# Reordering a planned kernel: layer 2 of the first pair ahead of layer 0's last pass, priorities in time, and quarter sums made by transfers

## The chip, the cores and the metric

The kernel runs on one core of a Trainium2 chip. The metric is device time in microseconds (us) of one execution, as a median of several. A core has a matrix engine (TensorE, PE in the profile; its weight loads are PEld), three engines for element-wise work (VectorE = DVE, ScalarE = ACT, GpSimd = POOL) and SyncE (SP), which in this kernel issues transfers. Each engine works off its own list of instructions in order and waits for others by semaphores. Transfers that SP issues and transfers that POOL issues stand in two separate queues and share 16 DMA engines.

## The reference

Four graph layers over x (8 batches x 2048 nodes x 64 channels) and one row-normalised adjacency matrix A (2048 x 2048, f32); each layer's output is added to its input and normalised over the channels. Cut to what matters:

```python
# layer 0: Chebyshev products, weights by node
y1 = A @ x;  y2 = 2 * (A @ y1) - x
out = sum over k in 0..2, d in 0..15 of emb[n, d] * ([x, y1, y2][k] @ w[d, k]) + bias
# layer 1: graph attention
e = leaky_relu(s1[:, None] + s2[None, :]);  e = where(A > 0.5, e, -9e15)
out = elu(softmax(e) @ x)
# layer 2
out = ((A + I) @ (x @ W.T + b)) / rowsum(A + I)
# layer 3: v = x with node 0 set to a constant, then three times
v = relu([v, A @ v] @ W1.T + b1) @ W2.T + b2
```

Attention is a dense 2048 x 2048 softmax for each batch, so its element-wise work is large; the products with A are 2048 x 2048 by 512 columns each.

## The kernel before, in words

**Tiling.** The 8 batches make 4 *pairs* p = 0..3 of two batches, 128 columns of x each. A pair's x lies in SBUF as `SX[p]`, 16 node tiles of 128 x 128. Three more slots of that size, `SA`, `SB` and `SH`, hold y1, then u, h and results; `SH` holds layer 0's weights first. A product with A is a *sweep*: for each of 4 column chunks `c` (512 nodes) and 8 steps `q`, a tile `a` (128 x 2 x 512, 512 KB) of the transposed A is loaded, and two matmuls of 512 columns are accumulated on a PSUM bank `acc` (L1093). So a sweep is 32 tiles and 64 matmuls of a pair. SP issues the tile loads in the fixed order of the list `order_of_a` through a ring of six buffers (`fetch`, L234 to L245); `plus` takes tiles with the identity added, for layer 2.

**Stages.** Layer 0: `first_product` gives y1, `second_product` gives y2 (evicted by `y2_evict`), and `second_pass` (L576) does the matmuls with all 16 weight blocks (yp, L601), which `add_terms` (L613) weighs and sums on ACT and DVE; `first_norm` ends it. The sweep of pair 0's and 1's first products also makes the 0/-9e15 masks of A, which are stored (`by_col`, `by_row`). Layer 1: `layer1` and `scores` (L700) find the largest score of each row, `weights` (L798) makes the exponentials for one node tile: an add on DVE (L809), leaky ReLU on ACT (L817), an add on DVE (L822), an exp on ACT (L825), and then the matmul with x on PE (po, L836). POOL loads the masks for it (`mk`, `mr`). `finish` (L853, matmul pf L870) divides, applies elu and normalises; half 0 is staged and copied to `SX` by a POOL transfer. Layer 2: a sweep `layer2_product`, evicted to z by `z_evict` (L942, L945), then for each chunk `layer2_tail` (ps_emb L981 on PE, adds L990 and L994 on DVE), `start_chunk` (norm, transpose ps_vT L1015 into `SH`) and `u_chunk` (ps_u L1028, into `u_of(p, s)`). These tails wait in a queue, `queue2`, which `tails` works off in order. Layer 3: three sweeps over u, each with one seed matmul a chunk (L1082) and a relu eviction (`h_evict`, L951), then `u_chunk` or, in the end, `last_chunk` (ps_v L1048) and `store` (L1064).

**Joint layers.** Pairs 2 and 3 go together. `joint_layer2` (L1188) uses each `a` tile for both pairs; `sums` (L1159) meanwhile adds quarters of A on DVE (L1172: four sums s1..s4 of 8 tiles each, 32 adds), stored by POOL (L1174, `s<-s`), with some plain tiles loaded again (`pure`). `joint_layer3` (L1247) multiplies the 2x2 blocks of A by the two pairs' u with seven block products in place of eight: `sums_of_u` makes sums of u, `combine` sums of the results, the matmuls are L1299.

**What sets the order.** No loop nest does: the class `Plan` (L38) interleaves generators ("threads"). A thread yields an engine and what it waits for; `go` picks the thread that could begin first by the plan's own estimates of time, ties by rank, and lets it emit its next instructions. For PE a thread is taken to begin `SLACK` = 1.0 us later than its inputs are there. The order so found is fixed in each engine's list when the program is built. `sweeps` (L1404) is the thread of the products: first products of pairs 0 and 1; then for each pair its second product (with the next pair's first product beside it); then for pairs 0 and 1 layer 2 and three steps of layer 3; then the joint layers. `tails` starts once pair 3 has left layer 0:

```python
def tails():
    yield "PE", [("x1", NPAIR - 1)]
    for n in range(NPAIR * 4 * NCH):
        yield "PE", [("q2", n + 1)]
        yield from queue2[n]()
```

Attention of pairs 0, 1, 2, 3 runs beside all this from about 400 us on: the masks' first load is issued at 396.7 us, the last at 1603.1.

Of the kernel before, what the change touches and what calls it, by code (L numbers as in the profile page):

```python
# [12 lines left out]
ALU = mybir.AluOpType  # L13
# [24 lines left out]
class Plan:  # L38
# [7 lines left out]
    SLACK = 1.0  # L46
# [27 lines left out]
    def start(self, rank, gen):  # L74
        try:
            self.threads.append([rank, next(self.count), gen, next(gen)])
        except StopIteration:
            pass
# [11 lines left out]
    def go(self):  # L90
        while self.threads:
            best = min(
                self.threads,
                key=lambda th: (self.begins(th)[0], (*th[3][2:], th[0])[0], th[1]),
            )
            t, _, eng = self.begins(best)
            assert t < NEVER, [th[3] for th in self.threads]
            try:
                best[3] = best[2].send(eng)
            except StopIteration:  # L100
                self.threads.remove(best)
# [42 lines left out]
def resnorm_d4_kernel(  # L144
# [60 lines left out]
    def batches(v):  # L205

        if len(v.shape) == 3:
            v = v.rearrange("p t n -> p (t n)")
        return v.rearrange("p (b c) -> p b c", c=C)

# [116 lines left out]
    for e in range(2):  # L327
# [20 lines left out]
        for m in ("s1", "s2", "s3", "s4")  # L348
# [73 lines left out]
    def rows_of_adj():  # L422


        for t in range(NT):
            yield "SP", [115.0 + 9.0 * t, bc_ring]
# [3 lines left out]
            done = plan.dma("SP", 1024, bc_ring.t, 115.0 + 9.0 * t)  # L430
            plan.start(1, row_tile(t, an, k, done))

    def row_tile(t, an, k, done):
# [15 lines left out]
        if all(("by_row", i) in at for i in range(NT)):  # L449
            at["rows"] = done  # L450
# [125 lines left out]
    def second_pass():  # L576

        for n in range(NPAIR * NCH):
# [32 lines left out]
            xg_ring.give(kx, t_pe)  # L611

# [46 lines left out]
    def layer1(p):  # L659
# [38 lines left out]
        plan.start(10 + p, scores(p, sv, xc, s_rows, done))  # L698

    def scores(p, sv, xc, s_rows, done):  # L700
        s2b = []
        for e in range(2):
            yield "DMA", [bc_ring, done, "rows"]
# [228 lines left out]
    JOINT = (NPAIR - 2, NPAIR - 1)  # L932
    SH_of = {p: SH for p in range(NPAIR)}

    def after_l2(p):
        return SB if p == 0 else SX[p - 1] if p < NPAIR - 1 else SX[0]

    def u_of(p, s):

        return SX[p] if s == 1 else SB if p == NPAIR - 1 else SA  # L940

    def z_evict(p, c, pa, give, done):  # L942
# [4 lines left out]
        give(done)  # L947
# [23 lines left out]
    def tails():  # L971
        yield "PE", [("x1", NPAIR - 1)]
# [28 lines left out]
    def start_chunk(p, c, v, done):  # L1001
# [10 lines left out]
        yield "PE", [done, pp_ring]  # L1012
# [11 lines left out]
    def u_chunk(p, c, w, dst, bias, s, done):  # L1024
        yield "PE", [done, pp_ring]
# [48 lines left out]
    def sweep(*products, masks=False):  # L1074

        for c in range(NCH):
            pas = []
            for source, evict, need, before, seed in products:
                yield "PE", [acc_ring, *before(c)]
                pas.append(acc_ring.take([P, CW], "acc"))  # L1080
                if seed:
                    nc.tensor.matmul(  # L1082
                        pas[-1][0], lhsT=seed, rhs=SH[:, tiles(c), :], start=True, stop=False
# [44 lines left out]

    RQ = AQ // 2

    def quarters(k, r):

        return [(k, r), (k, r + RQ), (k + 2, r), (k + 2, r + RQ)]

    def order_of_joint():
        for k in range(2):
            for r in range(RQ):
                order_of_a.extend((c, q, True) for c, q in quarters(k, r))
        for s in range(3):
            for m in ("a11", "a12", "s2", "s3", "a22", "s1", "s4"):  # L1140
                i, j = {"a11": (0, 0), "a12": (0, 1), "a22": (1, 1)}.get(m, (0, 0))
                for k in range(2):
                    for r in range(RQ):
                        if m[0] == "a":
                            order_of_a.append((k + 2 * i, r + RQ * j, False))
                        else:
                            order_of_a.append((m, (k, r), False))

    def pure(k, r):

        yield "SP", [("group", k, r), *([xg_ring] if len(xg_ring.freed) > 1 else [NEVER])]
        got = []
        for c, q in (quarters(k, r)[i] for i in (0, 3)):
            t, kt = xg_ring.take([P, 2, CW], "pure")
            nc.sync.dma_start(t, tile_of_adj(c, q))
            got.append((t, kt, plan.dma("SP", 512, xg_ring.t)))
        return got

    def sums(k, r, taken):  # L1159

        tiles4 = [(t, kt, got) for t, kt, got, _ in taken]
        own = {}
        if r // 2 == k:
            own = dict(zip((0, 3), (yield from pure(k, r))))
        a11, a12, a21, a22 = ((own.get(i) or tiles4[i])[0] for i in range(4))
        ready = [(own.get(i) or tiles4[i])[2] for i in range(4)]

        def out_of(m, a, b, op, *after):
            yield "DVE", [bc_ring, *after]
            t, kt = bc_ring.take([P, 2, HALF], m)  # L1170
            t = t.rearrange("p a b -> p (a b)")[:, 0 : 2 * CW].rearrange("p (t n) -> p t n", n=CW)
            nc.vector.tensor_tensor(t, a, b, op)  # L1172
            done = plan.run("DVE", dve(2 * CW), *after)
            nc.gpsimd.dma_start(sum_tiles[m][k, r], t)  # L1174
            bc_ring.give(kt, plan.dma("DMA", 512, done))
            return t, done

        s3, d3 = yield from out_of("s3", a11, a21, ALU.subtract, ready[0], ready[2])
        s1, d1 = yield from out_of("s1", a21, a22, ALU.add, ready[2], ready[3])
        s2, d2 = yield from out_of("s2", s1, a11, ALU.subtract, d1)  # L1180
        s4, d4 = yield from out_of("s4", a12, s2, ALU.subtract, d2)
        for (_, kt, _, free), d in zip(taken, (d2, d4, d1, d1)):
            a_ring.give(kt, max(free, d))
        for _, kt, _ in own.values():
            xg_ring.give(kt, d2)
        refill()

    def joint_layer2():  # L1188
        p, o = JOINT
        at["group", 0, 0] = 0.0  # L1190
        for k in range(2):
            pas = {}
            for r in range(RQ):
                taken = []
                for i, (c, q) in enumerate(quarters(k, r)):
                    n = next(used)
                    if r == 0 and i in (0, 2):
                        if i == 0:
                            yield "PE", [po_ring, ("x2", p), ("x2", o)]
                            t2, kp = po_ring.take([P, 2, CW], "po")  # L1200
                            pas[c] = [(t2[:, e, :], kp) for e in range(2)]
                        else:
                            pas[c] = []
                            for e in range(2):
                                yield "PE", [acc_ring]
                                pas[c].append(acc_ring.take([P, CW], "acc"))
                    for e, pair in enumerate(JOINT):
                        yield "PE", [("a", n)]
                        t, kt = a_tiles[n]
                        for b in range(2):  # L1210
                            m = 2 * q + b
                            nc.tensor.matmul(
                                pas[c][e][0],
                                lhsT=SX[pair][:, m, :],
                                rhs=t[:, b, :],
                                start=(r == 0 and i in (0, 2) and b == 0),
                                stop=(r == RQ - 1 and i in (1, 3) and b == 1),
                            )
                        done = plan.run("PE", mm(CW, 2), ("a", n))
                        if r == RQ - 1 and i in (1, 3):  # L1220
                            if i == 3:
                                give = lambda t, kk=pas[c][e][1]: acc_ring.give(kk, t)
                            else:
                                give = give_half(pas[c][e][1])
                            plan.start(1, z_evict(pair, c, pas[c][e][0], give, done))
                    del a_tiles[n]
                    taken.append((t, kt, at["a", n], done))
                    if i == 0:
                        nxt = (k, r + 1) if r + 1 < RQ else (k + 1, 0)
                        at[("group", *nxt)] = plan.free["PE"]  # L1230
                    spent[0] += 1
                plan.start(5, sums(k, r, taken))
                refill()

    halves_left = {}

    def give_half(kp):
        def give(t):
            left, last = halves_left.pop(kp, (2, 0.0))
            if left == 1:  # L1240
                po_ring.give(kp, max(t, last))
            else:
                halves_left[kp] = (1, max(t, last))

        return give

    def joint_layer3():  # L1247
        p, o = JOINT
        U, _ = e_ring.take([P, 2, HALF], "u23")
        T12, _ = e_ring.take([P, 2, HALF], "t12")  # L1250
        T34, _ = e_ring.take([P, 2, HALF], "t34")
        T = [
            t[:, i, :].rearrange("p (t n) -> p t n", n=P) for t in (T12, T34) for i in range(2)
        ]
        for s in range(3):
            up, uo = u_of(p, s), u_of(o, s)
            B11, B21, B12, B22 = up[:, 0:8], up[:, 8:16], uo[:, 0:8], uo[:, 8:16]
            plan.start(0, sums_of_u(s, T, B11, B21, B12, B22))
            u = lambda pair, half: lambda k: ("u", pair, s, 2 * half + k)
            t = lambda i: lambda k: ("t", s, i, k)  # L1260
            seed = gv if s else w31v
            held = {}
# [215 lines left out]
```

## Time and profile before

The times are 2131.99, 2132.62 and 2137.06 us. The page is of one execution of its own:

| | |
|---|---|
| median of 3 runs | 2132.62 us |
| the profiled execution, its time | 2133.99 us |
| its span (first to last instruction) | 2132.2 us |
| mean granted TensorE clock in it | 0.994 |
| PE busy | 97% of the span |
| DVE, ACT, POOL busy | 70%, 46%, 10% |
| moved by transfers | 495.85 MB, mean 233 GB/s |

How to read it: the page's first part gives each engine's busy time, share and number of instructions; its second cuts the span in 40 slices of 53.3 us with one digit each (tenths busy; for PEclk tenths of the full clock). A window line gives, for a stretch of the span, the busy us of each engine in it, the granted clock, the share of the DMA engines' time and GB/s. A wait line names the waiting engine and its line, the engine and line that released it, and the total, number and longest of these waits. A transfer's line ends with the median time from issue to landing. A busy PE is not PE at its peak, and the engines' names of tiles are the program's.

### The profile page before, as it was taken

The page shows a single profiled execution, that of the slowest core. Times are in us where ns is not written, and L with a number is a line of the kernel's source. Part 1 is how long each engine was busy: PE and PEld are TensorE (multiplying, and loading weights), DVE is VectorE, ACT ScalarE, POOL GpSimd, SP SyncE. Part 2 cuts the span into 40 slices and gives each one's busy share as a digit, 9 for nine tenths or more (in the row PEclk, how much of TensorE's full clock was granted, in tenths as well). Part 3 has the DMA queues.
Part 4 walks back from the last instruction along what each step waited for, and adds up shares of the span by engine and source line. Part 5 has one row for each costly group of instructions (what it writes and reads, how often), then busy time and mean ns, then how long its engine had stood idle before and what let it go on. Part 6 is the DMA issues. An engine that isn't in the chain of part 4 may idle for free. (4 is left out here: it accounts for less than half of the span.)

```text
span 2132.2 us, 19037 instructions
## 1 busy us (share of the span) xinstructions
PE 2067.3 (97%) x6325; PEld 914.9 (43%) x6325; DVE 1496.4 (70%) x1908; ACT 974.9 (46%) x1794; POOL 213.0 (10%) x374
## 2 busy tenths in 40 slices
PE   8999999999999999999798999989999999999998
PEld 3444444433433443433343453443444444444444
DVE  2226647998799999789998979999796455120214
ACT  0025424567776566777624857336575012000002
POOL 2310000100110100000010101011010110000000
PEclk9999999999999999999899999999999999999999
DMA  9799835634443465554388778897776777878785
GB/s 303 267 333 345 306 105 209 218 122 136 138 137 131 159 238 169 170 178 150 124 309 299 254 267 285 279 339 239 264 236 234 290 255 273 280 254 281 251 288 188
DMA packets 208740, 495.85 MB, mean 233 GB/s; under 512 B 20274, under 2 KB 28594, under 8 KB 204530
## 3 DMA queue, kind: packets, MB, share of 16 engines
q1 hardware_dynamic: 165058, 347.62, 48.0%
q0 software_dynamic: 39360, 144.92, 19.7%
q10 hardware_dynamic: 4224, 2.10, 0.4%
q8 instruction: 50, 0.82, 0.2%
q14 instruction: 48, 0.39, 0.1%
HBM read 446.14 MB, written 46.33 MB: 231 GB/s over the span
## 5 line engine op out<-in xcount | busy, mean ns | idle before, releaser
L1093 PE MATMUL acc<-a,SX 128*128 128x512 f32 x1024 | 465.8, 598 | 9.6 <-DMA SX<-in_x 6.6
L1093 PE MATMUL acc<-a,SA 128*128 128x512 f32 x768 | 348.6, 596 | 13.1 <-DMA a<-in_adj_t 12.4
L817 ACT ACTIVATE e<-e,sv 128x1024 f32<-128x1024 f32 x256 | 280.1, 1154 | 114.4 <-DVE e L809 110.6
L731 DVE CUSTOM_DVE_ANT_0 junk<-s2b,mr 128x2048 bf16<-128x2048 f32 x128 | 292.7, 2287 | 5.2 <-DMA mr<-by_row 3.9
L624 ACT ACTIVATE terms<-yp,emb_sb 128x128 f32<-128x128 f32 x896 | 243.5, 400 | 113.6 <-PE yp L601 113.3
L1093 PEld LDWEIGHTS acc<-a,SX 128*128 128x128 f32 x1024 | 190.3, 191 | 242.2 <-issue 229.6
L822 DVE TENSOR_TENSOR e<-e,mb 128x2048 f32<-128x2048 f32 x128 | 290.0, 2286 | 6.0 <-ACT e L817 5.4
L809 DVE TENSOR_TENSOR e<-s1b,mk 128x2048 f32<-128x2048 f32 x128 | 289.1, 2286 | 6.5 <-PE po L836 4.0
L825 ACT ACTIVATE e<-e 128x2048 f32<-128x2048 f32 x128 | 245.0, 1928 | 67.5 <-DVE e L822 67.2
L601 PE MATMUL yp<-SH,xgT 128*128 128x512 f32 x512 | 246.9, 607 | 3.3 <-ACT sv L358 3.3
L836 PE MATMUL po<-e,SX 128*64 128x512 f32 x1024 | 235.4, 602 | 3.1 <-ACT e L825 3.1
L1093 PEld LDWEIGHTS acc<-a,SA 128*128 128x128 f32 x768 | 140.9, 190 | 186.0 <-issue 166.0
L1299 PE MATMUL acc<-a,t 128*128 128x512 f32 x384 | 168.7, 592 | 0.0
L636 DVE TENSOR_TENSOR terms<-terms 128x512 f32<-128x512 f32 (+1 forms) x176 | 130.0, 738 | 42.2 <-ACT terms L624 38.2
L601 PEld LDWEIGHTS yp<-SH,xgT 128*128 128x128 f32 x512 | 90.9, 189 | 145.7 <-issue 137.6
L836 PEld LDWEIGHTS po<-e,SX 128*64 128x64 f32 x1024 | 68.1, 137 | 155.8 <-issue 133.7
L601 PE MATMUL yp<-SH,y2T 64*128 64x512 f32 x512 | 128.3, 617 | 0.0
L804 POOL DMA_DIRECT2D mk<-by_col x128 | 69.0, 540 | 546.7 <-DVE e L809 452.1
L1093 PE MATMUL acc<-a,SB 128*128 128x512 f32 x256 | 118.3, 595 | 0.0
L1299 PEld LDWEIGHTS acc<-a,t 128*128 128x128 f32 x384 | 72.0, 190 | 86.1 <-issue 86.1
L601 PEld LDWEIGHTS yp<-SH,y2T 64*128 64x128 f32 x512 | 43.6, 186 | 79.9 <-issue 76.4
L1093 PEld LDWEIGHTS acc<-a,SB 128*128 128x128 f32 x256 | 47.2, 190 | 57.3 <-issue 57.3
(225 smaller groups left out, 1677.7 us busy)
## 6 DMA issues: line engine op xcount, KB each, us to landing
a<-in_adj_t SPq DMA_DIRECT2D x496, 512.0 KB, 5.5
a<-s SPq DMA_DIRECT2D x96, 512.0 KB, 4.5
mr<-by_row POOLq DMA_DIRECT2D x64, 512.0 KB, 5.9
mk<-by_col POOLq DMA_DIRECT2D x128, 256.0 KB, 5.0
an<-in_adj SPq DMA_DIRECT2D x16, 1024.0 KB, 10.7
s<-s POOLq DMA_DIRECT2D x32, 512.0 KB, 5.0
a<-a_plus_i SPq DMA_DIRECT2D x24, 512.0 KB, 5.0
by_col<-mk POOLq DMA_DIRECT2D x32, 256.0 KB, 5.8
```

What stands on the lines that cost most here:

```text
L601: nc.tensor.matmul(yp[:, e, :], lhsT=y2T[rows, cs] if k2 else xg[:, e, cs], rhs=(wk2 if k2 else w01)[rows, hs], start=(k2 == h), stop=(k2 ...
L624: nc.scalar.activation(batches(terms[0][:, dd, :]), term, AF.Copy, scale=weight)
L636: nc.vector.tensor_tensor(a, a, b, ALU.add)
L731: nc.vector.tensor_tensor_reduce(out=junk, in0=s2b[e][0], in1=masks[t][0], scale=1.0, scalar=LOWEST, op0=ALU.add, op1=ALU.max, accum_out=m ...
L804: nc.gpsimd.dma_start(mk, by_col[jt // 2][:, jt % 2, h * HALF : (h + 1) * HALF])
L809: nc.vector.tensor_tensor(e, s1b[0], mk.unsqueeze(1).to_broadcast([P, 2, HALF]), ALU.add)
L817: nc.scalar.activation(e[:, i, :], e[:, i, :], AF.Prelu, bias=sv[:, 2 + i, jt : jt + 1], alpha=ALPHA)
L822: nc.vector.tensor_tensor(e, e, mb[0], ALU.add)
L825: nc.scalar.activation(e, e, AF.Exp)
L836: nc.tensor.matmul(po[i * C : (i + 1) * C, f, :], lhsT=SX[p][:, t, i * C : (i + 1) * C], rhs=e[:, i, f * CW : (f + 1) * CW], start=(t == 0 ...
L1093: nc.tensor.matmul(pa, lhsT=source[:, m, :], rhs=t[:, i, :], start=(m == 0 and not seed), stop=(m == NT - 1),)
L1299: nc.tensor.matmul(pa, lhsT=B[:, 2 * r + b, :], rhs=at_[:, b, :], start=(r == 0 and b == 0 and not go_on), stop=(r == RQ - 1 and b == 1), ...
```

## The change

- **Planner.** `SLACK` is 0.0. A table `BACK` adds a time to a thread's beginning when the next one is chosen (below zero: it goes ahead): `add_terms` of pair 0 by -3.02, `finish` by -0.48, `scores` of pair 2 by -0.01. `scores` gets rank 1.2 for pair 0 and 9.5 + p else, and no longer waits for all rows' masks. The loads of A's rows begin at 120 in place of 115 on the plan's clock.
- **Layer 2 of pair 0** goes ahead of the second product of pair 3. `tails` waits for nothing at its start. Pair 0 gets other slots: its `SH_of` is `SX[0]`, its u goes to `SB`, `SH` and `SB` for the three steps, its layer 2 result to `SA`, with waits until these are free (`x1 used`, `y1 used`, `w0 used`).
- **Joint layer 2** is gone: pairs 2 and 3 have plain sweeps, each loading its own tiles.
- **Quarter sums** (sa = a12 + a22, sb = a11 + a12, sc = sa + a11, sd = sc + a21) are made from DRAM to DRAM by transfers of POOL, planned from 320 us on with 14 us between them: for each of 8 tiles a copy, then a transfer that adds to what is there.
- **Joint layer 3** uses another scheme of seven products on these sums; two products go on in a bank that already holds another, one seed is added to a bank after DVE has read it, and some sums of u are made in place. The matmuls are now at L1219, the seeds at L1203.

```diff
-    SLACK = 1.0
+    SLACK = 0.0
+    BACK = {
+        ("add_terms", 0): -3.02,
+        ("finish", None): -0.48,
+        ("scores", 2): -0.01,
+    }
...
-                key=lambda th: (self.begins(th)[0], (*th[3][2:], th[0])[0], th[1]),
+                key=lambda th: (self.begins(th)[0] + th[4], (*th[3][2:], th[0])[0], th[1]),
...
-            yield "SP", [115.0 + 9.0 * t, bc_ring]
+            yield "SP", [120.0 + 9.0 * t, bc_ring]
...
-        plan.start(10 + p, scores(p, sv, xc, s_rows, done))
+        plan.start(1.2 if p == 0 else 9.5 + p, scores(p, sv, xc, s_rows, done))
...
-            yield "DMA", [bc_ring, done, "rows"]
+            yield "DMA", [bc_ring, done]
...
-    JOINT = (NPAIR - 2, NPAIR - 1)
-    SH_of = {p: SH for p in range(NPAIR)}
+    JOINT = (NPAIR - 1, NPAIR - 2)
+    SH_of = {p: SH if p else SX[0] for p in range(NPAIR)}
     def after_l2(p):
-        return SB if p == 0 else SX[p - 1] if p < NPAIR - 1 else SX[0]
+        return SA if p == 0 else SX[p - 1] if p < NPAIR - 1 else SX[0]
     def u_of(p, s):
-        return SX[p] if s == 1 else SB if p == NPAIR - 1 else SA
+        if s == 1:
+            return SX[p] if p else SH
+        return SB if p in (0, 1, NPAIR - 1) else SA
...
     def tails():
-        yield "PE", [("x1", NPAIR - 1)]
...
     def u_chunk(p, c, w, dst, bias, s, done):
-        yield "PE", [done, pp_ring]
+        room = {0: ["y1 used"], 1: ["w0 used"]}.get(s, []) if p == 0 else []
+        yield "PE", [done, pp_ring, *room]
...
+    QUARTER = {"a11": (0, 0), "a12": (0, RQ), "a21": (2, 0), "a22": (2, RQ)}
+    def sums_of_a():
+        n = itertools.count()
+        for m, a, b in (
+            ("sa", "a12", "a22"),
+            ("sb", "a11", "a12"),
+            ("sc", "sa", "a11"),
+            ("sd", "sc", "a21"),
+        ):
+            for x in (a, b):
+                for k, r in sum_tiles[m]:
+                    if x in QUARTER:
+                        part = tile_of_adj(k + QUARTER[x][0], r + QUARTER[x][1])
+                    else:
+                        part = sum_tiles[x][k, r]
+                    before = [("sum", m, k, r)] if x == b else []
+                    if x not in QUARTER:
+                        before.append(("sum", x, k, r, True))
+                    yield "DMA", [320.0 + 14.0 * next(n), *before]
+                    nc.gpsimd.dma_start(
+                        sum_tiles[m][k, r], part, **({"accum_op": ALU.add} if x == b else {})
+                    )
...
-    def sums(k, r, taken):
...
-            nc.vector.tensor_tensor(t, a, b, op)
-            nc.gpsimd.dma_start(sum_tiles[m][k, r], t)
...
-    def joint_layer2():
...
+            def z_and_v(s, k, pa, ka, done):
+                yield "DVE", [done, ("x", s, k)]
+                nc.vector.tensor_tensor(half(Z, k), half(X, k), pa, ALU.subtract)
+                at["z", s, k] = done = plan.run("DVE", dve(CW), done)
+                yield "PE", [done]
+                seeded(p, 2 + k, pa, False)
+                done = plan.free["PE"] + plan.LAG
+                yield "DVE", [done]
+                nc.vector.tensor_tensor(half(V, k), pa, half(X, k), ALU.subtract)
+                at["v", s, k] = done = plan.run("DVE", dve(CW), done)
+                acc_ring.give(ka, done)
...
     def sweeps():
...
         for p in range(NPAIR):
             products = [second_product(p)]
             if 0 < p < NPAIR - 1:
                 products.append(first_product(p + 1))
+            if p == NPAIR - 1:
+                yield from sweep(layer2_product(0))
+                at["x1 used"] = 0.0
             yield from sweep(*products)
+        at["y1 used"] = 0.0
         for p in range(NPAIR - 2):
-            yield from sweep(layer2_product(p))
+            if p:
+                yield from sweep(layer2_product(p))
             for s in range(3):
                 yield from sweep(layer3_product(p, s))
+        yield from sweep(layer2_product(NPAIR - 2))
...
-        yield from joint_layer2()
+        yield from sweep(layer2_product(NPAIR - 1))
         yield from joint_layer3()
```

## The prediction

> **What bounds the kernel now.** I read the page's busy shares first, then its slices, then the windows where PE is not full, then the waits in these windows.
>
> ```profile
> PE 2067.3 (97%) x6325; PEld 914.9 (43%) x6325; DVE 1496.4 (70%) x1908; ACT 974.9 (46%) x1794; POOL 213.0 (10%) x374
> PE   8999999999999999999798999989999999999998
> PEclk9999999999999999999899999999999999999999
> ```
>
> PE is busy for 97% of the 2132.2 us span, so the change can win only from PE's 65 idle us, from its slow clock, or by less PE work. Slice 20 (index from 1; 53.3 us each, so 1013 to 1066) is the weakest, and the clock falls there too. The windows give the size (columns: window, length, busy us of PE, PEld, DVE, ACT and POOL with counts, granted clock, DMA share, GB/s):
>
> ```profile
> 350.00:1000.00 650.00, 646.99 (x1993) 263.92 (x1993) 599.05 (x670) 443.23 (x980) 68.21 (x124) 1.00 0.50 165
> 1000.00:1025.00 25.00, 21.93 (x64) 8.15 (x62) 24.76 (x23) 19.16 (x33) 2.68 (x5) 1.00 0.56 181
> 1025.00:1050.00 25.00, 12.98 (x62) 7.23 (x60) 24.38 (x48) 14.39 (x25) 0.93 (x2) 0.73 0.18 61
> 1100.00:1150.00 50.00, 42.80 (x122) 18.98 (x120) 41.98 (x47) 14.13 (x17) 7.67 (x14) 1.00 0.98 359
> 1400.00:1450.00 50.00, 43.35 (x127) 19.08 (x127) 47.27 (x40) 19.00 (x22) 9.29 (x17) 1.00 0.96 341
> 1700.00:1750.00 50.00, 45.52 (x164) 24.62 (x163) 29.08 (x56) 11.42 (x28) 6.39 (x12) 1.00 0.68 249
> 1750.00:1800.00 50.00, 46.46 (x166) 24.71 (x165) 28.68 (x57) 11.15 (x27) 4.26 (x8) 1.00 0.76 263
> ```
>
> From 350 to 1000 PE loses 3 us in 650: no gain is to be had there. From 1000 to 1050 it idles 3.07 + 12.02 = 15.1 us, from 1700 to 1800 it idles 8.0. The two windows at 341 and 359 GB/s idle 7.2 and 6.7. Waits of PE from 1000 to 1060, then from 1675 to 1800 (total us, times, longest):
>
> ```profile
> PE ps_vT L1015 <- DVE v L1007: 7.4, 1, 7.4
> PE ps_emb L981 <- DVE SB L990: 3.5, 2, 2.9
> PE acc L1093 <- ACT z L945: 3.1, 1, 3.1
> PE po L836 <- ACT e L825: 1.1, 1, 1.1
> ```
>
> ```profile
> PE ps_vT L1015 <- DVE SX L510: 5.1, 5, 1.6
> PE ps_emb L981 <- ACT z L945: 1.3, 2, 0.7
> L1172 DVE TENSOR_TENSOR s<-a,s x8: 1218/1226/1226, 1665.4 to 1793.1; 128x1024 f32<-128x1024 f32 x8
> ```
>
> The first hole: layer 2's product of pair 0 has just ended, layer 3 can't start before its tail (ps_emb, norm, ps_vT, ps_u), and that tail stands on DVE, 98% busy with attention's 2.29-us adds. The second: layer 2's tails of pairs 2 and 3 come together, behind the quarter sums of the last line on DVE. The 1100 and 1400 windows wait for `a` tiles (5.2 and 4.9 us).
>
> **Part 1: layer 2 of pair 0 ahead of layer 0's last pass.** PE's work is the same: 64 matmuls of 512 columns (0.858 us each, two records of 429 ns), their 32 `a` loads on SP move ahead of the 32 of the last pass in one ring, and DVE gets four tails, an estimated 4 us each from the end tail's rows (four 0.69-us steps and four of 0.17), between 731 and 945 us; 350 to 1000 has 51 us of DVE free. To place things in the changed order I priced each of PE's instructions by its duration in this trace and added up; positions are such estimates. The moved sweep stands at 731 to 807; the last pass of layer 0, with the yp matmuls mixed in, runs from 809 to 945. So the tail that starved PE has 138 us of cover. This removes 7.4 + 3.5 + 3.1 + 1.1 = **-15.1 us**.
>
> The slow clock goes with it. The row: 12.98 us busy at 0.73, so 12.98 x 0.27 = 3.5 us lost. The rule (the Trainium skill, "TensorE: Matmul & The Clock Gate", Part 1): after an idle window of about 3.4 us the clock halves until about 3.4 us of work have passed; that is 1.7 us for the one wait over 3.4 us, 1.8 us less gain. I take the row, **-3.5**.
>
> What is late next? (a) x2 of pair 0: its last pf stands at 703.5, the first tile of its last quarter is needed at 742.3, 38 us later; in the trace that chain (pf at 749.6 to the last norm at 773) took 24. Cover 14 us. (b) u of pair 0 goes to SB, which y1 of pair 3 occupies to the end of the last pass at 945: all four ps_u come right behind it, and layer 3 right behind them at 949.5. A copy of u takes 0.59 (ACT) or 0.69 (DVE), a ps_u 4 x 0.22; chunk 0's copy hides behind the next ps_u, the last ones may show. (c) SH holds the weights until the yps end at 1037.7; u of step 1 wants it at 1042.6, 5 us cover. Between 0 and 4 us, by the copies in (b): **+2**. If DVE or ACT stands in a 2.3-us add when each comes, (b) costs as much as the old hole's first two waits, 10.9: a rival below.
>
> **Part 2: quarter sums off DVE, and two plain layer 2 sweeps for the shared one.** 32 adds of 1.22 us leave DVE (39 us, all between 1661 and 1793), and the tails of pair 2 get their place within pair 3's sweep, so those bunched together no more. The idle 8.0 us plus 0.7 from 1675 to 1700: **-8.7**. The last sweep starts at 1630, 15 us behind the last pf of pair 3, with no long DVE adds then: its chain's own DVE and ACT steps (hp 0.69, min 0.42, exp and norm) sum to an estimated 7. Its 64 matmuls run to 1694 and need 32 loads of 0.52 MB in 64 us, 262 GB/s; 1750 to 1800 carried 263.
>
> The transfers are moved to 320 to 1200 us: 32 copies and 32 accumulating DMAs, one every 14 us, on POOL, beside:
>
> ```profile
> q0 software_dynamic: 39360, 144.92, 19.7%
> a<-in_adj_t SPq DMA_DIRECT2D x496, 512.0 KB, 5.5
> mk<-by_col POOLq DMA_DIRECT2D x128, 256.0 KB, 5.0
> an<-in_adj SPq DMA_DIRECT2D x16, 1024.0 KB, 10.7
> s<-s POOLq DMA_DIRECT2D x32, 512.0 KB, 5.0
> ```
>
> No accumulating DMA is in this trace. By the nearest row, the sums' own stores, one takes 5.0 us. The rule against (the Trainium skill, "Collectives: The Full Stack", "The bandwidth ceiling: the fold count and why AG ≠ RS ≠ AR"): an add done by transfers needs two source reads, so it goes at about half the rate of a copy; that makes 10 us, near the 1 MB row's 10.7. By the first the transfers move 33.5 MB, by the second 50.3 MB; over 900 us 37 or 56 GB/s onto 165: hidden until 1000 by either. Where 359 GB/s were moved, 56 x 50 us = 2.8 MB would cost 7.8 us by the rule, 5.2 by the row. Issues: 64 x 0.7 us (by_col's row, 708 ns) on an engine 10% busy. They replace 16.8 MB of stores and 4.2 MB of re-loads, the 32 extra `a` loads add 16.8. Eight copies go before eight accumulates, 112 us apart, so POOL doesn't stand waiting for a copy. Mask loads behind an accumulate have three buffers: two tiles ahead are 2 x 4.57 = 9.1 us of DVE (L809 and L822), against 5.0 to land. Bounds 0 and 7.8 (a gain is excluded: bytes are only added here): I take **+2**, as only the last groups reach a full stretch.
>
> **Part 3: joint layer 3 rewritten.** Still 7 x 16 matmuls and 8 seeds a step; 22 DVE steps of 0.69 for 22. New is a seed that PE issues only after z is made by DVE from the same bank: it stands 1.72 us behind its product's end, and needs 0.1 + 0.69 + 0.1. Behind it queue the next product's matmuls. **0**, hidden by that 1.72-us step; without cover 6 x 1 us.
>
> **Part 4: the planner** (SLACK 1.0 to 0, three starts drawn forward, scores' rank). PE's instructions may now stand up to 1 us earlier against their inputs. Over the whole span PE's waits for ACT in layers 0 and 1 were 3.1 us (po for exp, 3 times), 3.3 (yp) and 3.3 (ps_y). Most exps lead their po by 2.5 to 5 us, so few cross. Low end -2 (PE instructions that no longer stand back), high end these 9.7 once more: **+3**, a third of it, by the leads.
>
> **Sum** on the profiled span: 2132.2 - 15.1 - 3.5 - 8.7 + 2 + 2 + 0 + 3 = 2111.9. The profiled execution took 2133.99, 1.8 beside its span; the median of the runs, 2132.62, is 1.4 lower: 2111.9 + 1.8 - 1.4 = 2112.3, say **2112**. With all three unknowns at their low ends (-2 + 0 + 0 for 7) it is 2103; with all at their high ends (9.7 + 7.8 + 4) 2127, unlikely together: its own range is 2103 to 2122.
>
> **Rivals.**
> - The hole only moves: 10.9 us appear at 945 (ps_u behind a DVE in long adds) or x2 of pair 0 is over 14 us late: 2112 - 2 + 10.9 = 2121. For it: DVE is 92% busy there. Against: copies may go to ACT, 68% busy.
> - Better: the two stretches that wait for `a` lose their waits too, since work is mixed otherwise: 7.2 + 6.7 = 13.9, so 2098. Against: bytes rise, not fall.
> - No change: without slack every second of the 128 pairs of exps makes PE wait 0.3 us, 19 us for the 3 taken: 2128. For it: PE sits at 99% from 350 to 1000, with nothing left to hide in. Against: the leads.
> - Slower: accumulates hold q0 longer than masks can spare. 24 of them fall between 350 and 1000. One that takes T delays the mask behind it by T - 9.1, and DVE has 51 us free: the loss is 24 (T - 9.1) - 51. It decides where that eats the 20 us gained, at T = 12.1; at 13 us it is 42.6, so 2112 + 43 = 2155. For it: one queue, 10 by the rule already. Against: even so 9.1 nearly covers 10.
>
> **How the numbers follow.** Likeliest 0.57 (2112), hole moves 0.13 (2121), better 0.08 (2098), no change 0.10 (2128), slower 0.12 (2155). Under about 0.3% (6.4 us) a measurement of this kernel can't tell a change from none: faster is below 2126, which takes the first three, 0.78; same 0.10; slower 0.12. The range must leave out 0.2: the slower case goes, and half of the better; 2098 to 2136.
>
> **What would show it.** Right: around the end of layer 0 (950 to 1050) PE busy over 24 of each 25 us at clock 1.00, no ps_vT wait on DVE over 2 us; 1650 to 1750 with ps_vT waits under 1.5 in sum; DVE busy about 39 us less; from 350 to 1000 still over 99% PE. Wrong: po waiting for exp by more than 10 us in all (no slack), DVE waiting for mk loads (accumulates), or PE waits for SX of pair 0 near 740 or for SB near 945 of over 5 us.

## The result and the profile after

The changed kernel takes 2098.26 us (2095.41 to 2100.21), against 2132.3 for the kernel before beside it: 0.9827 times, 95% interval 0.9811 to 0.9843. That is 34 to 37 us less, where the forecast, 2112, was 20.6 less. The sign was right, the size too small. By the ratio, the time is 2132.62 x 0.9827 = 2095.7, below the 2098 at which my range ended; the rival at 2098 came nearest.

The page of the changed kernel, the same lines as shown of before:

```profile
span 2097.3 us, 19052 instructions
PE 2065.0 (98%) x6325; PEld 917.1 (44%) x6325; DVE 1461.5 (70%) x1873; ACT 989.0 (47%) x1797; POOL 257.6 (12%) x406
PE   8999999999999999999999999998999999999997
PEclk9999999999999999999999999999999999999999
```

PE has the same 6325 instructions and nearly the same busy time (2065.0 for 2067.3); DVE has 35 us less. The dip at 1013 to 1066 us is gone, in PE's row and in the clock's. The windows (columns as before: window, length, busy us with counts of PE, PEld, DVE, ACT and POOL, clock, DMA share, GB/s):

```profile
350.00:1000.00 650.00, 648.39 (x2028) 271.25 (x2027) 606.24 (x682) 431.17 (x912) 112.71 (x175) 1.00 0.71 215
1000.00:1025.00 25.00, 24.64 (x64) 10.19 (x64) 24.49 (x29) 5.52 (x19) 3.18 (x6) 1.00 0.97 350
1025.00:1050.00 25.00, 25.00 (x62) 10.67 (x60) 24.55 (x26) 5.74 (x18) 3.35 (x6) 1.00 0.91 328
1100.00:1150.00 50.00, 50.00 (x182) 21.23 (x181) 37.71 (x24) 35.72 (x32) 10.78 (x15) 1.00 0.92 290
1400.00:1450.00 50.00, 45.74 (x125) 20.92 (x123) 48.66 (x52) 8.12 (x13) 8.75 (x16) 1.00 0.99 369
1700.00:1750.00 50.00, 50.00 (x168) 26.23 (x167) 15.15 (x38) 9.54 (x22) 0.00 (x0) 1.00 0.82 265
1750.00:1800.00 50.00, 50.00 (x144) 24.30 (x143) 8.41 (x18) 5.66 (x12) 0.00 (x0) 1.00 0.80 264
```

Both holes closed, and so did the one from 1100 to 1150, which I had left open in the sum; its twin at 1400 stayed. All the waits of PE that are left over 0.8 us, whole span, of the changed kernel:

```profile
PE acc L1106 <- DMA a<-in_adj_t: 8.0, 6, 2.4
PE acc L1106 <- DMA SX<-in_x: 6.5, 1, 6.5
PE ps_w L417 <- ACT w32d L407: 3.9, 1, 3.9
PE ps_v L1061 <- ACT h_o L964: 1.5, 1, 1.5
```

**Where the time went.** PE's work is the same in both kernels, so a table of what PE *lost* adds up. For each PE instruction I took its start in the trace less the summed work of all PE instructions ahead of it (0.858 us a matmul of 512 columns, 0.45 for a po, and so on, the same in all kernels); the growth of that difference over a stretch is what PE lost there, by waiting or by a slow clock. Each column is one profiled execution. The columns to the right are experiments told below.

| stretch, us | before | after | move alone | third part alone | move + third part, old planner | after, shared sweep |
|---|---|---|---|---|---|---|
| 0 to 350 | 16.8 | 21.4 | 18.7 | 21.5 | 15.9 | 20.6 |
| 350 to 1000 | 17.3 | 15.5 | 20.6 | 18.5 | 14.4 | 15.5 |
| 1000 to 1100 | 19.7 | 2.6 | 3.6 | 19.6 | 2.2 | 2.6 |
| 1100 to 1400 | 12.4 | 3.0 | 6.7 | 22.4 | 9.1 | 3.0 |
| 1400 to 1450 | 8.5 | 6.9 | 7.8 | 6.2 | 8.2 | 6.7 |
| 1450 to 1600 | 1.7 | 1.6 | 1.4 | 1.5 | 1.5 | 2.5 |
| 1600 to 1850 | 11.9 | 1.0 | 23.1 | 0.8 | 0.6 | 33.4 |

Before less after is 36.2; the tail behind the last ps_v is 1.3 longer after, which leaves the 34.9 by which the span fell. Up to 250 us executions with the same code there differ by up to 5 us (10.4 to 15.2 lost among the changed kernel and its variants), so the first row tells little by itself.

### The profile page after: what moved, and what is told of

Read it like the earlier page. It is cut to its first block, busy times and chain, and to the rows that moved or that the text cites. A ratio compares the mean times of both kernels' runs of the same rounds, so it can differ in the third digit from the quotient of the medians.

```text
span 2097.3 us, 19052 instructions
## 1 busy us (share of the span) xinstructions
PE 2065.0 (98%) x6325; PEld 917.1 (44%) x6325; DVE 1461.5 (70%) x1873; ACT 989.0 (47%) x1797; POOL 257.6 (12%) x406
## 4 chain that ended last, share of the span: by engine, by line
PE 88%; issue 5%; DVE 4%; DMA 2%; ACT 0%; POOL 0%; POOLq 0%; ACTq 0%; DVEq 0%
PE acc L1106 44%; PE yp L609 15%; PE po L845 11%; PE acc L1219 11%; DVE junk L740 2%; PE ps_u L1041 2%; DMA a<-in_adj_t 2%; PE acc L1095 1%; PE acc L1203 1%; DVE terms L645 1%; PE pf L879 1%; PE ps_emb L991 1%; PE ps_sv L690 1%; PE ps_v L1061 0%; PE ps_xT L680 0%
## 5 line engine op out<-in xcount | busy, mean ns | idle before, releaser
L1106 PE MATMUL acc<-a,SX 128*128 128x512 f32 x1152 | 523.7, 600 | 12.5 <-DMA SX<-in_x 6.5
L1106 PE MATMUL acc<-a,SB 128*128 128x512 f32 x768 | 348.6, 597 | 0.4 <-DMA a<-in_adj_t 0.4
L1106 PEld LDWEIGHTS acc<-a,SX 128*128 128x128 f32 x1152 | 214.5, 192 | 276.9 <-issue 259.2
L831 DVE TENSOR_TENSOR e<-e,mb 128x2048 f32<-128x2048 f32 x128 | 290.4, 2286 | 19.9 <-ACT e L826 19.2
L1106 PEld LDWEIGHTS acc<-a,SB 128*128 128x128 f32 x768 | 142.1, 191 | 170.3 <-issue 168.4
L645 DVE TENSOR_TENSOR terms<-terms 128x512 f32<-128x512 f32 (+1 forms) x176 | 130.0, 739 | 18.5 <-ACT terms L633 14.1
L1106 PE MATMUL acc<-a,SA 128*128 128x512 f32 x256 | 117.6, 594 | 1.6 <-DMA a<-in_adj_t 1.6
L1219 PE MATMUL acc<-a,t 128*128 128x512 f32 x192 | 85.4, 592 | 0.0
L636 DVE SCALAR_TENSOR_TENSOR terms<-yp,emb_sb,terms 128x128 f32<-128x128 f32 x128 | 34.6, 344 | 54.8 <-PE yp L609 41.4
L1106 PEld LDWEIGHTS acc<-a,SA 128*128 128x128 f32 x256 | 47.1, 190 | 58.2 <-issue 54.3
```

The lines of the kernel that those rows point to most:

```text
L645: nc.vector.tensor_tensor(a, a, b, ALU.add)
L831: nc.vector.tensor_tensor(e, e, mb[0], ALU.add)
L1106: nc.tensor.matmul(pa, lhsT=source[:, m, :], rhs=t[:, i, :], start=(m == 0 and not seed), stop=(m == NT - 1),)
L1219: nc.tensor.matmul(pa, lhsT=B[:, 2 * r + b, :], rhs=at_[:, b, :], start=(start and r == 0 and b == 0), stop=(r == RQ - 1 and b == 1), skip ...
```

## The experiments

A ratio is to the kernel before, run in the same round on the same chip. Its medians differ by some us from round to round (2132.3 to 2136.6), so runs of different rounds compare best by their ratios.

**The move alone, and the rest without the move.** Theory A: the move only fills the hole. Theory B: it also takes away the wait near 1100. For the first run, the hunks of part 1 of the change go onto the kernel before; for the second, they are taken out of the changed kernel:

```diff
+            if p == NPAIR - 1:
+                yield from sweep(layer2_product(0))
+                at["x1 used"] = 0.0
             yield from sweep(*products)
...
         for p in range(NPAIR - 2):
-            yield from sweep(layer2_product(p))
+            if p:
+                yield from sweep(layer2_product(p))
```

> The kernel before with one part of the change: layer 2 of pair 0 ahead of the last pass, with its slots. Theory A (the move removes only the hole at the end of layer 0): 18.5 us less, so about 2114, and the waits for a tiles near 1100 and 1400 us stay at about 5 us each. Theory B (the move also brings pair 2's scores, with their mask rows, beside the yp matmuls, and so ends the wait near 1100): about 2106, with one such wait left, near 1400.

2127.64 us, ratio 0.9960 (0.9947 to 0.9973). Neither figure came: the hole is filled (19.7 to 3.6 in the table) and near 1100 nothing is lost any more (0.4 from 1100 to 1150, for 8.5), as theory B has it, but the time fell by 9 us and not by 27. (Of the 32 scores of pair 2 on DVE, 20 run beside the yp matmuls here, which last to 1102 us; in the kernel before 2 do, with yp ending at 1003.) The table shows where the rest is: 1600 to 1850 lost 23.1 in place of 11.9, and 350 to 1000 lost 3.3 more. PE's waits from 1600 to 1800 in this run:

```profile
PE ps_vT L1017 <- DVE SX L510: 5.1, 5, 1.6
PE po L1215 <- DVE SX L510: 4.3, 1, 4.3
PE acc L1215 <- DMA a<-in_adj_t: 2.4, 1, 2.4
```

The second is new: the shared layer 2 sweep (L1215) stands waiting for the norm that ends pair 3's attention. The last exp of attention ends at 1626.9 us in the kernel before and at 1625.0 here: PE reached the end of its other work sooner, attention hardly did. DVE is busy for 93% of the time between 350 us and its last attention add (92% in the kernel before), which leaves that end little room to move. So of the 17.6 us that PE had gained by 1600 (the rows above, before less move alone), 11.2 were given back after it.

> The changed kernel with layer 2 of pair 0 put back behind the last pass, in its old slots. Theory A: the hole returns (18.5 us), about 2117, and no wait for a tiles near 1100. Theory B: the hole and the wait near 1100 return, 26 to 27 us, about 2125. Rival (the planner's values fill the hole without the move): under 2105.

2152.2 us, ratio 1.0071 (1.0053 to 1.0090): slower than the kernel before, and no theory's figure. The trace has one wait that explains the excess:

```profile
PE ps_rows L793 <- DVE mx L763: 38.6, 1, 38.6
```

Here the planner had put the transpose of a pair's greatest scores on PE's list ahead of work that was ready, and PE stood behind it. So this run doesn't price the move by itself; it shows that these planner values don't suit the old order of sweeps.

**The planner's values.** The planner of before in the changed kernel (SLACK, the table, the ranks, the wait for all rows, 115 for 120):

> The changed kernel with the planner of before: SLACK 1.0, no table of starts, the old ranks of scores and their wait for all mask rows, adjacency rows from 115. My forecast's price for the planner (3 us lost): about 2095. Planner worth nothing: 2098. Planner brings the end of the wait near 1100: about 2106.

2100.7 us, ratio 0.9834 (0.9819 to 0.9848), beside 0.9827 (0.9811 to 0.9843): not told apart. On balance the planner's values are worth nothing to 0.2%, for which I had booked a loss of 3 us. The table shows two effects in that nothing: the new values cost 5.5 us before 350 (a wait that is told below under the better version) and save 6.1 from 1100 to 1400 and 1.3 at 1400. With the old values PE still waits for `a` tiles near 1100:

```profile
1100.00:1150.00 50.00, 47.22 (x149) 21.07 (x149) 49.23 (x46) 26.99 (x29) 8.31 (x13) 1.00 1.02 339
```

**The joint stage, from both sides.** The move and the new planner values on the old joint layers (SLACK at 0.6, and scores waiting for all rows):

> The kernel before with the move and the new planner values, SLACK at 0.6, and scores still waiting for all mask rows; joint layers 2 and 3 and the quarter sums on DVE as before. If the separate sweeps and the sums by transfers are worth what PE lost between 1650 and 1800 (11.4 us): about 2110, with ps_vT waiting for norms in that stretch. If the sums by transfers cost something before it: under 2107.

2156.04 us, ratio 1.0089 (1.0072 to 1.0106): 46 us over what was expected. PE waits 19.2 us for exps, in the whole span, and 52.3 us are lost after 1600:

```profile
PE po L846 <- ACT e L835: 19.2, 6, 4.8
```

The last exp ends at 1663.2 us here, and the shared sweep comes behind it. In the changed kernel the last exp comes nearly as late, at 1654.6, 28 us later than in the kernel before, and PE loses 1.0 us. That made theory C: what the third part is worth is not the adds that it takes from DVE, but that a plain sweep of pair 2 gives PE 55 us of work (64 x 0.858) which doesn't need pair 3's attention. Theory D: it is the adds. The move alone, with the 32 adds and their stores left out:

```diff
-            nc.vector.tensor_tensor(t, a, b, op)
             done = plan.run("DVE", dve(2 * CW), *after)
-            nc.gpsimd.dma_start(sum_tiles[m][k, r], t)
```

> The kernel before with the move, without the 32 sum adds on DVE and their stores; tiles of A stand in for the sums, so pairs 2 and 3 are not the reference's at the end. Theory C (the stretch after 1630 waits because the shared sweep needs pair 3's attention, which ends by DVE's work whatever PE does): at least 12 of the 23 us lost between 1600 and 1800 stay, so no more than 10 below the move alone. Theory D (the adds on DVE cause the loss there): about 20 below the move alone.

2120.98 us, ratio 0.9933 (0.9919 to 0.9948): 6.7 below the move alone by medians, 5.8 by the ratios. Of the 23.1 lost after 1600, 16.9 stay, the wait of 4.3 for SX among them. Theory C holds, and the adds are a smaller part. From the other side, the changed kernel with a shared sweep, everything else kept:

```diff
-        yield from sweep(layer2_product(NPAIR - 2))
...
-        yield from sweep(layer2_product(NPAIR - 1))
+        yield from sweep(layer2_product(NPAIR - 2), layer2_product(NPAIR - 1))
```

> The changed kernel with one shared sweep for layer 2 of pairs 2 and 3 (each tile of A used for both, 32 loads fewer), the sums still by transfers. Theory C: PE stands before the shared sweep until x2 of pair 3 is there, 15 us or more above the changed kernel. Theory D: within 5 us of it.

2130.43 us, ratio 0.9977 (0.9967 to 0.9987). One edit of the order takes back 32 us of the gain (0.9977 less 0.9827 of 2132), though 32 loads fewer are made. Its window from 1600 to 1650 and its waits in there:

```profile
1600.00:1650.00 50.00, 31.63 (x105) 9.47 (x105) 45.74 (x27) 42.70 (x35) 4.54 (x8) 0.80 0.28 85
```

```profile
PE po L845 <- ACT e L834: 18.4, 6, 6.8
```

PE has nothing left but po, and so goes at attention's pace, with DVE busy for 45.7 of the 50 us and ACT for 42.7; the clock falls to 0.80 besides. In the changed kernel the same 50 us have DVE at 47.1 and PE at 50.00.

**The third part alone.** Plain sweeps, sums by transfers and the new joint layer 3; no move, the old planner:

> The kernel before with the third part alone: plain layer 2 sweeps of pairs 2 and 3, sums by transfers, the rewritten joint layer 3; no move, the old planner. The hole at the end of layer 0 is as before. If the parts add up by PE's losses: 11.4 less than before, about 2121. If this part is worth what it was on top of the move (27): about 2106. If the planner's old values leave the hole larger: over 2125.

2134.9 us, ratio 1.0000 (0.9991 to 1.0010). It closes the end (11.9 to 0.8 in the table), and loses as much elsewhere, most of it from 1100 to 1400:

```profile
1100.00:1150.00 50.00, 40.83 (x111) 18.10 (x109) 46.24 (x53) 14.17 (x22) 12.82 (x19) 0.93 1.04 360
```

```profile
PE acc L1097 <- DMA a<-in_adj_t: 14.3, 9, 2.8
```

The waits are those from 1100 to 1300, for `a` tiles, 5.2 in the kernel before. POOL issues accumulating transfers in just that stretch (1110.9 to 1212.6 us). The changed kernel issues the same ones at the same time (1117.2 to 1211.3) and loses 3.0 there, so they are not enough to make this loss; whether it needs them no run shows. So the move is worth 9 us by itself, the third part nothing, and both with the old planner 36: the parts are not a sum.

**The price of the transfers.** Left out, and issued twice:

> The changed kernel without the 32 copies and 32 accumulating transfers; the last layer's products load tiles of A in place of the sums, so its values for pairs 2 and 3 are not the reference's, and the order on PE, DVE and ACT is that of the changed kernel. My forecast's price for the transfers (2 us): 2 us below the changed kernel. Hidden wholly: the same within 2 us. At the upper end of my bound: 8 us below.

2096.95 us, ratio 0.9828 (0.9810 to 0.9846): no difference from the changed kernel.

> The changed kernel with each copy and each accumulating transfer issued a second time, onto tiles that nobody reads. If the sums are hidden with room to spare: within 5 us of the changed kernel. If POOL's queue is the limit (masks late by what an accumulate takes beyond 9.1 us): 20 us or more above it, DVE waiting for mk.

2116.43 us, ratio 0.9914 (0.9899 to 0.9929): 18 us above it. The cover is not deep. PE's waits for `a` tiles grow from 8.0 to 18.3 us, and DVE waits 15.0 us for masks, for 0.7 in the changed kernel: the mechanism of my slower rival (waits in this run):

```profile
PE acc L1111 <- DMA a<-in_adj_t: 18.3, 14, 2.3
DVE junk L745 <- DMA mr<-by_row: 10.0, 3, 7.9
DVE e L823 <- DMA mk<-by_col: 5.0, 3, 2.1
```

One transfer's time to landing, from the changed kernel's list of transfers (of these the adding ones are those from in_adj_t; for sa and sb the list has copies and adds in one row):

```profile
sc<-sa POOLq DMA_DIRECT2D x8, 512.0 KB, 7.0
sc<-in_adj_t POOLq DMA_DIRECT2D x8, 512.0 KB, 10.0
sd<-sc POOLq DMA_DIRECT2D x8, 512.0 KB, 6.0
sd<-in_adj_t POOLq DMA_DIRECT2D x8, 512.0 KB, 9.9
```

Over all four sums the trace's medians are 8.7 us for the 32 adds (7.3 to 21.7) and 6.1 for the 32 copies.

**The waits near 1100 and 1400.** First theory: the mask rows of scores (512 KB for 4.6 us of DVE) beside a sweep. Pairs 2 and 3 load every second row only; the greatest score is but a shift, which the softmax cancels:

```diff
+            if p >= 2 and t % 2:
+                yield "DMA", [("mask", p, t - 1)]
+                masks[t] = kept[t - 1]
```

> The changed kernel in which pairs 2 and 3 load only every second mask row for scores and use it twice, so their attention is not the reference's; DVE's work is the same. Theory (the loss near 1400 us, 6.9, comes from mask rows of 512 KB beside a sweep with nothing else on PE): that loss falls under 2 us, about 2092. Rival (the sweep's own loads are too slow there): it stays, about 2098.

2097.32 us, ratio 0.9820 (0.9804 to 0.9837); 6.0 us are still lost at 1400, for 6.9.

> The same on the kernel before: the losses near 1100 and 1400 us, 8.5 each, should both fall under 2. If PE's time alone counts: 17 less, about 2116. By theory C (pair 3's attention ends by DVE's work near 1627, and the shared sweep stands behind it): a part comes back as loss after 1600, no more than 12 less, 2121 or more.

2134.44 us, ratio 0.9995 (0.9986 to 1.0004); 7.9 and 7.5 are still lost. The theory fell. Two other edits: fewer bytes from another load of that stretch, and other work for PE in it. One of the two 1 MB rows less:

> The changed kernel with pair 3's first shift row (mb, 1 MB spread over the partitions) not loaded; the row s1b stands in for it, which the softmax cancels. The order on PE is that of the changed kernel. Theory (the loss near 1400 us comes from the two 1 MB loads that fall together beside a sweep without other PE work): it falls from 6.9 to 4 or less, 2095. Rival (mask rows or the sweep's own rate): it stays, 2098.

2095.35 us, ratio 0.9810 (0.9792 to 0.9829), with 4.6 lost from 1400 to 1450 for 6.9. And pair 3's scores ahead of pair 2's weights:

```diff
-        plan.start(1.2 if p == 0 else 9.5 + p, scores(p, sv, xc, s_rows, done))
+        plan.start((1.2, 10.5, 11.5, 10.5)[p], scores(p, sv, xc, s_rows, done))
```

> The changed kernel with scores of pair 3 ranked ahead of pair 2's weights (10.5 for 12.5), meant to take pair 3's mask rows away from the sweep near 1400 us. If it does so and DVE's order costs nothing else: 2092. If pair 2's weights come late instead, PE waits for exps: above 2100.

2101.1 us, ratio 0.9840 (0.9824 to 0.9855). The loss at 1400 is gone (0.7), since po now stands between the sweep's matmuls there and 207 to 249 GB/s are moved from 1400 to 1440 in place of 296 to 406; but 7.1 us are lost after 1650, and the sum is no better. What these four runs agree with: by its matmuls' times, a sweep alone on PE eats a tile of 0.52 MB each 1.72 us, 305 GB/s; scores, unlike weights, give PE nothing to do between, and whatever else is loaded then tips it over. How much each load adds isn't settled.

**A version that beats both.** From 250 to 300 us the changed kernel loses 7.5 us, for 1.3 in the kernel before, by one wait, ps_w for w32d (3.9), behind which the clock falls to 0.66 (window 290 to 300). The wait came with the planner's new values: no run with the old ones has it. Placing that step later on the plan's clock:

```diff
-        yield "PE", [pp_ring, done]
+        yield "PE", [pp_ring, done + 8.0]
         pw, k = pp_ring.take([P, CW], "ps_w")
```

> The changed kernel with one wait moved: the second step of the layer 3 weights (ps_w) is placed 8 us later, so that PE doesn't stand 3.9 us behind ACT at 290 us, where the clock falls to 0.66 after it. If both go: 3.9 and about 3 us less, 2091 to 2093. If DVE decides there (layer 1 of pair 0 begins by DVE's work): 2098.

2092.97 us (2090.1 to 2093.06), ratio 0.9797 (0.9782 to 0.9812): 5.3 us below the changed kernel by medians, 6.4 by the ratios, whose intervals just touch. The window from 290 to 300 has PE busy throughout and the clock whole, and 1.3 us are lost from 250 to 300 in place of 7.5:

```profile
290.00:300.00 10.00, 10.00 (x33) 5.08 (x32) 8.71 (x22) 5.09 (x11) 2.94 (x3) 1.00 0.78 258
```

## Why the prediction was right and wrong

- **The hole at the end of layer 0** (-15.1 - 3.5 + 2 = -16.6): 19.7 to 2.6 lost from 1000 to 1100, so -17.1. Right. Row and rule for the slow clock differ by 1.8, too little for this total to tell; the wait that I feared at ps_u (+2, and 10.9 in the rival) didn't show: PE's waits from 900 to 1060 in the changed kernel are 0.4 us.
- **The end of layer 2** (-8.7): measured -10.9. My sum took the idle time only; PE lost some 3 us there that no idle row shows. The size was near by luck, since the reason was not the one at work: I gave it to the adds on DVE and to bunched tails. On top of the move, the third part is worth 27 us (2127.64 to 2100.7), of which the adds are about 6; most of the rest is that the plain sweep doesn't wait for pair 3's attention. In the kernel before this was hidden, as I read it, since the hole held PE back until attention was nearly done.
- **The sum transfers** (+2, bounds 0 and 7.8): 0 by the run without them. The time to landing, 8.7 (9.9 and 10.0 for the last two sums), was nearer the 10 that I estimated from the rule of two source reads (the Trainium skill, "Collectives: The Full Stack", "The bandwidth ceiling: the fold count and why AG ≠ RS ≠ AR") than the 5.0 of the row that I set beside it, though 1.4 times a copy's 6.1 and not twice; it was hidden all the same. In another order the upper bound may be real: the third part alone loses 10.0 more from 1100 to 1400.
- **The planner** (+3, bounds -2 and +9.7): nothing to be told on balance, -2.4 by medians. po waits for exp nowhere in the list of the changed kernel, so the cost that I feared did not come; another did, at ps_w (5.5 more before 350 us than with the old values), and 7.4 less at the waits for tiles makes up for it.
- **The step that failed**: the sum has no term for the two stretches in which PE waits for `a` tiles. (The kernel before idles 7.2 us in the one near 1100, at 359 GB/s, and 6.7 in the one near 1400, at 341; the prediction has the two in the other order.) The rival "Better" named them, and I set it at 0.08 because "bytes rise, not fall". But from 1100 to 1400 9.4 us less are lost, with more bytes moved in all (525 MB for 496). The move alone brought 5.7 of them (12.4 to 6.7). On top of the move the third part with the old planner has 9.1, and the planner's new values take that to 3.0. What the runs point to is not the bytes of the whole but what PE has to do beside the sweep. The po matmuls between 1100 and 1150 us, in the kernel before, the move alone and the changed kernel (us, count, then clock, DMA share and GB/s as before):

```profile
1100.00:1150.00 50.00, 1.98 (x10) 1.00 0.98 359
1100.00:1150.00 50.00, 7.31 (x32) 1.00 0.79 265
1100.00:1150.00 50.00, 18.27 (x80) 1.00 0.92 290
```

All sixteen kernels fit this. With 56 to 88 po in these 50 us 1.0 us or less is lost there, also in the run without the move; with 32 it is 0.4 twice and 4.2 once (the old planner, with sum transfers beside); with 12 or fewer, 7.9 to 14.3. The po stand there because pair 2's scores come earlier: in the changed kernel all 32 run between 965 and 1048 us, beside yp matmuls, which leave a tile more time, and po can follow; in the kernel before 27 of them run from 1070 to 1202. That reading is argued from where things stand; of the edits made near 1400, only the one that put po there took such a loss away. The loss near 1400 itself, the other half of the rival, fell by 1.6 only.

- Not foreseen: +4.6 before 350 us (+6.2 at the ps_w wait, the rest within what the first 250 us vary), +1.3 in the tail, -1.8 from 350 to 1000.

Added up: -17.1 - 10.9 - 9.4 - 1.6 - 0.1 - 1.8 + 4.6 + 1.3 = -35.0 of the span. My sum had -16.6 - 8.7 + 2 + 3 = -20.3. The miss of 14.7 is 11.0 for the two waits for tiles, 5.0 for the penalties of transfers and planner, which don't show on balance, 2.2 at the end of layer 2, 2.4 in small change (0.5, 1.8 and 0.1), less 5.9 lost at both ends of the span.

Of the rivals, "slower" named a mechanism that is there (masks waiting behind accumulating transfers) and only shows at twice the transfers. "The hole only moves" did happen, to the move alone: not at 945 where I looked for it, but 650 us later, at the next place where PE needs attention's end. I worked out the move's worth from the stretch where the hole was, and did not ask what PE would meet when it came 17.6 us sooner. (The range was to leave out 0.2; the slower case and half of the better are 0.16.)

## What to carry to other kernels

When two engines run side by side for long, a hole filled on one is a gain only if the other's chain isn't what the next stage waits for: look up when that chain ends and what work stands between. Here the order that lets PE do 55 us of other work behind attention was worth more (32 us, by the run that takes it back) than the adds taken away (about 6). Price parts of a change together where one makes the cover of the other: alone they gave 9 and 0 us, together 36.

## What the runs showed of the hardware

- An accumulating transfer of 512 KB between DRAM tensors took 8.7 us to land in the changed kernel, a plain one 6.1 (medians of 32; 9.9 to 10.0 and 6.0 to 7.0 for the last two sums). POOL spent 1.13 us issuing the first and 0.50 to 0.71 on the second (medians).
- A PE wait of 3.9 us cost 6.2 in all (7.5 to 1.3 lost from 250 to 300): the granted clock was 0.66 in the 10 us around its end. In the shared sweep's run, waits of up to 6.8 us brought it to 0.80 over 50 us.
- The core's DMA engines moved 393 to 406 GB/s from 1420 to 1450 us of the changed kernel, at whose end (1440 to 1450) PE waited 4.3 us for tiles; at 350 GB/s (1000 to 1025) PE still ran 24.64 of 25 us.
